# A deep four-layer block on one core: two groups of small matmuls widened from 32 and 56 rows to 128, with the added rows cleared on GpSimd

## Chip, core and metric

One Trainium2 chip, one of its cores. The metric is the device time of one execution of the whole program in microseconds (us); the number compared is the median of several executions.

## What is computed

The input is 16 images of 56 x 56 tokens with 128 channels, in fp32. Four layers follow one another, each as `x = x + layer(group_norm(x))`: a shifted-window attention (7 x 7 windows, 4 heads), a triangle multiplication, a Fourier operator with attention over planes, and a bilinear convolution. The change touches the last two.

In the Fourier layer the 56 image rows are treated as 56 planes. Attention weights between planes are made per head, and one part of the output is a mix of the planes with weights that all pixels share. In the code that is a 56 x 56 matrix `mt`, applied to every column of the image: for each column `j`, `y[:, j] = mt.T @ x[:, j]` for every channel.

In the bilinear layer the reference does this first:

```python
xp = jax.nn.silu(x @ W1) @ W2          # W1: 128 x 160, W2: 160 x 160
q = xp[..., :128]; k = xp[..., 128:144]; v = xp[..., 144:]
q, k, v = l2norm(q per head), l2norm(k), l2norm(v)
```

The 160 hidden channels do not fit 128 partitions, so the kernel holds them as a large part of 128 and a small part of 32. Then `k` and `v` go through grouped 3 x 7 convolutions, and three bilinear products of `q` with their results make the output.

## The kernel before

**Lanes and order.** The 16 images run in two lanes (even and odd images). Each lane has its own arena (128 x 17152 fp32 in SBUF), five `w2` buffers of 128 x 512, eight small ones of 128 x 64 (`sm`), two PSUM banks `psb` and one double bank `psd`. The program is written image by image with plain Python loops; the Tile framework's scheduler then lays the instructions of both lanes out on the engines, by its own timeline of their costs, and sets all waits. Each engine runs its instructions in that order. So a program that differs by a few instructions can be laid out differently throughout.

**The Fourier layer** (`_fourier`, `run` from L1141). After the attention (L1050 to L1133) comes a product with a table of spectral weights: 8 rounds of 8 steps, each step with two table transfers of 56 x 1344 issued by GpSimd (L1200), one product of 112 x 1344 on VectorE (L1202) and a group of matmuls (L368 and L371 are the lines of the helper `together`). Then the planes' product with the common weights: for 14 groups of four columns, four transposes on TensorE (L1235), an evacuation by ScalarE that also subtracts the mean (L1237, into 56 rows of a `w2` buffer), four matmuls with `mt` (L1240, 56 rows) and a copy back (L1241). `mt` is made at L1181. The inverse transforms and two spectral operators end the layer (L945 to L1021, L1245 to L1271).

**The bilinear layer** (`_bilinear`). An image is seven chunks of 448 tokens. `project(q)` (L1317 to L1371) normalizes a chunk on VectorE (L1320), multiplies with `W1` in two parts of 128 and 32 rows of output (L1324), applies Silu on ScalarE (L1325) into `ha` (128 rows) and `hb` (32 rows), and multiplies with `W2`: first for the 128 channels of `q`, over 128 rows (L1327) and over 32 rows (L1328), accumulating in PSUM; then, for four blocks of 112 tokens, for the 32 channels of `k` and `v`, over 128 rows (L1337) and over 32 rows (L1338), with the sums of squares per head next to them (L1339). The `q` part goes to DRAM eightfold (`dy`, L1313), and `k`, `v` after normalization go to a padded image in DRAM; its border comes from a clearing on GpSimd (L1360). `spread` (L1375) loads the padded image back, `conv` (L1389 and `together`) makes the convolutions, and `contract` reads `dy` back in replicated form (L1408), multiplies on VectorE (L1411) and sums on TensorE. Projections run two chunks ahead of their use.

GpSimd's queue holds the table transfers (L1200), clearings (L520, L526, L658, L973, L974, L1061, L1145, L1250, L1258, L1303, L1360), one copy between partitions per image (L1164) and the small pieces of the window attention's input (L536).

Of the kernel before, what the change touches and what calls it, by code (L numbers as in the profile page):

```python
# [42 lines left out]
P = 128  # L43
T = 56
# [3 lines left out]
CH = 448  # L48
# [156 lines left out]
def _weights(i):  # L205

    g = {k: np.asarray(v) for k, v in i.items()}
    w, early = {}, {}
    w["wqkv"] = g["L0_conv_w_qkv"]
    w["wout0"] = g["L0_conv_w_out"]  # L210
    w["bout0"] = g["L0_conv_b_out"][:, None]
    x, y = np.arange(WIN) // WS, np.arange(WIN) % WS
    pb = g["L0_conv_pos_emb"][x[None] - x[:, None] + WS - 1, y[None] - y[:, None] + WS - 1]
    pos = np.zeros((P, WIN), np.float32)
    pos[:WIN] = pb
    pos[64 : 64 + WIN] = pb
    early["pos"] = pos

    pw, gw = g["L1_conv_p_in_w"].T, g["L1_conv_g_in_w"].T
    cut = [slice(0, 64), slice(128, 192)], [slice(64, 128), slice(192, 256)]  # L220
    for n, (a, b) in zip("ab", cut):
        w["w1" + n] = np.concatenate([pw[:, a], pw[:, b], gw[:, a], gw[:, b]], 1)
    w["pout"] = g["L1_conv_p_out_w"].T
    w["gout"] = g["L1_conv_g_out_w"].T
    names = ["ln_in_w", "ln_in_b", "ln_out_w", "ln_out_b"]
    w["ln"] = np.stack([g["L1_conv_" + n] for n in names], 1)

    rows = [e[0] for e in ENT]
    for n, key in (("a", "L2_conv_wQ"), ("b", "L2_conv_wK")):
        k = g[key][:, 0]  # L230
        s = np.concatenate([k[0][:, :12], k[1]], 1)
        for c, part in enumerate("ri"):
            e = s[..., c][:, rows].reshape(32, 32, 2, 8).transpose(2, 1, 0, 3)
            e = np.stack([e, e], 1)
            early[n + part] = e.reshape(P, 256)
            m = s[:, [t[0 if n == "a" else 1] for t in MIR], 0, c].T
            early[n + "m" + part] = np.concatenate([m, m, m, m], 0)
    wq, wk = g["L2_conv_wQs"][:, 0], g["L2_conv_wKs"][:, 0]

    def rep(v, n):  # L240
        return np.broadcast_to(v, (n,) + v.shape)

    early["wq"], early["wk"] = rep(wq, P), rep(wk, P)
    early["wqh"] = np.concatenate([rep(wq[:16], 64), rep(wq[16:], 64)], 0)
    early["wkh"] = np.concatenate([rep(wk[:16], 64), rep(wk[16:], 64)], 0)
    early["bq"] = rep(g["L2_conv_bQs"], P)
    head = np.array([[16 * (s % 2) + 2 * (s // 2) + hh for s in range(16)] for hh in range(2)])
    wv, wp = g["L2_conv_wVs"][:, 0], g["L2_conv_wPs"][0]
    early["wvp"] = np.repeat(wv[head], T, 0)
    early["wpp"] = np.repeat(wp[head], T, 0)  # L250
    early["cols"] = np.stack([wv, wp], 1)
    sc = [g["L2_conv_norm_g"], g["L2_conv_norm_b"]]
    sc += [g["L2_conv_" + n].reshape(-1) for n in ("wM0s", "bM0s", "wM1s", "bM1s", "bPs")]
    w["sc"] = rep(np.concatenate(sc), P)
    for n, key in (("w0", "L2_conv_wM0"), ("w1", "L2_conv_wM1")):
        k = g[key][:, 0, 0]
        s = np.concatenate([k[0][:24], k[1]], 0)
        for c, part in enumerate("ri"):
            w["m" + n + part] = np.concatenate([s[..., c], s[..., c]], 0)
    k = g["L2_conv_wP"][:, :, 0]  # L260
    s = np.concatenate([k[0][:, :24], k[1]], 1)
    v = np.zeros((32, T, 32, 2), np.float32)
    v[:, :16, :16] = g["L2_conv_wV"][0, 0]
    v[:, 40:, :16] = g["L2_conv_wV"][1, 0]
    neg = (-np.arange(T)) % T
    late = {}
    for c, part in enumerate("ri"):
        late["p" + part] = s[..., c].transpose(0, 2, 1).reshape(32, -1)
        late["v" + part] = v[..., c].transpose(0, 2, 1).reshape(32, -1)
        early["vm" + part] = v[:, neg, 0, c]  # L270

    w["l3w1"] = g["L3_conv_W1"]
    w["l3w2a"] = g["L3_conv_W2"][:128]
    w["l3w2b"] = g["L3_conv_W2"][128:]
    h1 = g["L3_conv_H1_w"].reshape(16, 16, 3, 7)
    h2, gg = g["L3_conv_H2_w"][:, 0], g["L3_conv_G_w"][:, 0]

    wk3, wg3 = (np.zeros((P, 4, 2, 4, 8), np.float32) for _ in range(2))  # L280
    wf3 = np.zeros((P, 4, 16, 8), np.float32)
    for u in range(16):
        rows = slice(u % 4 * 21, u % 4 * 21 + 21)
        wk3[rows, u // 4, :, u % 4] = h1[u].reshape(2, 8, 21).transpose(2, 0, 1)
        wg3[rows, u // 4, :, u % 4] = gg.reshape(2, 8, 21).transpose(2, 0, 1)
        wf3[rows, u // 4, :, u % 8] = h2.reshape(16, 21).T
    wk3[84] = g["L3_conv_P1"][0].reshape(4, 4, 2, 8).transpose(0, 2, 1, 3)
    wg3[84] = g["L3_conv_I"][0].reshape(4, 4, 2, 8).transpose(0, 2, 1, 3)
    for n, v in (("l3wk", wk3), ("l3wf", wf3), ("l3wg", wg3)):
        w[n] = v.reshape(P, -1)  # L290
    return w, early, late
# [437 lines left out]
def _fourier(env):  # L729
    e = _Env(env)  # L730
    nc, mm, tt, ts, ptt, act, C, W, bc = e.nc, e.mm, e.tt, e.ts, e.ptt, e.act, e.C, e.W, e.bc
# [409 lines left out]
    def run(b, xt):  # L1141
# [14 lines left out]
        for g in range(8):  # L1156
            p = e.psb()
# [16 lines left out]
        p = e.psb()  # L1174
# [3 lines left out]
        p = e.psb()  # L1178
        mm(p[:T, :T], lhsT=C("fold"), rhs=r[:TT, :T], start=True, stop=True)
        mt = e.sm()  # L1180
        stt(mt[:T, :T], p[:T, :T], scol[:T, 0:1], C("ident")[:T, :T], ALU.mult, ALU.add)  # L1181


# [4 lines left out]
        for q in range(8):  # L1188
            s = slice(q * STEP, (q + 1) * STEP)
# [6 lines left out]
            for two in range(8):  # L1196
# [8 lines left out]
                for p, k, m in ((pa, 0, 2 * STEP), (pb, 2 * STEP, STEP)):  # L1205
                    for half in (1, 0):
# [4 lines left out]
                                lhsT=at[:, pair % 8, pair // 8, :],  # L1211
                                rhs=prods[half][:, k : k + m],
                                start=two == 0,
                                stop=two == 7,
# [3 lines left out]
            c0, o = e.w2(), e.w2()  # L1218
# [4 lines left out]
            p = pb[:TT, 256 : 256 + STEP]  # L1223
# [8 lines left out]
        for g in range(T // 4):  # L1232
            p = e.psb()
            for i in range(4):
                nc.tensor.transpose(p[:T, i * P : (i + 1) * P], y3[:, 4 * g + i, :], C("ident"))  # L1235
            xj = e.w2()
            act(xj[:T, :], p[:T, :], AF.Identity, bias=less[:T])  # L1237
            p = e.psb()
            for i in range(4):
                mm(p[:, i * T : (i + 1) * T], lhsT=xj[:T, i * P : (i + 1) * P], rhs=mt[:T, :T], start=True, stop=True)  # L1240
            nc.scalar.copy(y3[:, 4 * g : 4 * g + 4, :], p[:, : 4 * T].rearrange("p (j t) -> p j t", t=T))  # L1241

        def residual(t0, p):
# [32 lines left out]
def _bilinear(env):  # L1276
    e = _Env(env)
    nc, mm, tt, ts, act, C, W, bc = e.nc, e.mm, e.tt, e.ts, e.act, e.C, e.W, e.bc
# [18 lines left out]
    def run(b, xt):  # L1297
# [12 lines left out]
        def kept(p):  # L1310

            t, d = e.w2(), e.dram()
            nc.scalar.copy(t[:, :CH], p[:, :CH])  # L1313
            nc.scalar.dma_start(out=d.rearrange("p (k t) -> p k t", k=8), in_=bc(t[:, :CH], 1, 8))
            return d

        def project(q):  # L1317

            xg = e.w2()
            ts(xg[:, :CH], xt[:, q * CH : (q + 1) * CH], nm, rs, ALU.add, ALU.mult)  # L1320
            ha, hb = e.w2(), e.w2()
            for t, o, m in ((ha, 0, 128), (hb, 128, 32)):
                p = e.psb()
                mm(p[:m, :CH], lhsT=W("l3w1")[:, o : o + m], rhs=xg[:, :CH], start=True, stop=True)  # L1324
                act(t[:m, :CH], p[:m, :CH], AF.Silu)  # L1325
            p = e.psb()
            mm(p[:, :CH], lhsT=W("l3w2a")[:, :P], rhs=ha[:, :CH], start=True, stop=False)  # L1327
            mm(p[:, :CH], lhsT=W("l3w2b")[:, :P], rhs=hb[:32, :CH], start=False, stop=True)  # L1328
            dq = kept(p)
            sq = e.w2()  # L1330
            act(sq[:, :CH], p[:, :CH], AF.Square)
# [1 line left out]
            p = e.psb()  # L1333
            for a in range(4):
                s = slice(a * TT, (a + 1) * TT)
                o = p[:TT, a * 32 : (a + 1) * 32]
                mm(o, lhsT=ha[:, s], rhs=W("l3w2a")[:, P:], start=True, stop=False)  # L1337
                mm(o, lhsT=hb[:32, s], rhs=W("l3w2b")[:, P:], start=False, stop=True)  # L1338
                mm(p[:TT, P + a * NH : P + (a + 1) * NH], lhsT=sq[:, s], rhs=C("heads"), start=True, stop=True)  # L1339
            sk = e.w2()  # L1340
            act(sk[:TT, :P], p[:TT, :P], AF.Square)
# [13 lines left out]
            p = e.psb()  # L1355
# [93 lines left out]


        queries, kern, feat = {q: project(q) for q in range(2)}, {}, {}
        spread(0, 0)
        for q in range(NCH + 4):
# [42 lines left out]
```

## Time and profile before

| | us |
|---|---|
| median of 3 runs | 13443.8 |
| lowest and highest of them | 13435.75, 13488.92 |
| the profiled execution, its own time | 13405.75 |
| span of the profiled execution, first to last instruction | 13403.8 |
| busy: TensorE, its weight loads, VectorE | 10585.8, 5860.7, 9623.6 |
| busy: ScalarE, GpSimd | 3845.7, 1426.4 |

The mean granted clock of TensorE was 0.847 of full speed. HBM moved 155 GB/s over the span. One pair of images (both lanes) takes about 1650 us, and the span shows that pattern eight times.

How to read it: PE is TensorE's matmuls, PEld its weight loads, which overlap them; DVE is VectorE, ACT ScalarE, POOL GpSimd, SP the queue that issues most transfers. A group's row gives the source line, the engine and operation, the output and inputs by name, for a matmul rows times columns of the stationary operand, the shape of the moving one, and the number of instructions; then the busy time in us, the mean of one in ns, the idle time of the engine just before them, and what ended most of it. An fp32 matmul appears as two instructions (two passes).

### The profile page before, as it was taken

What the parts mean: (1) busy time and instruction counts of PE and PEld (TensorE: products, weight loads), DVE (VectorE), ACT (ScalarE), POOL (GpSimd) and SP (SyncE); (2) the same over time, 40 slices, a digit from 0 to 9 for tenths busy, and PEclk for the clock granted to TensorE, in tenths of its full rate; (3) what the DMA queues carried; (4) which work ended last, traced back from release to release, by engine and by line L of the source; (5) the groups of instructions that cost most, each with busy time, mean ns of one, the idle gap of its engine ahead of it and who ended that gap; (6) DMA issues with size and microseconds to landing.
All of it is one profiled execution on the core that took longest, in us unless ns stands there. A gap on an engine that the chain in (4) does not pass through costs nothing. (4 is left out here: it accounts for less than half of the span.)

```text
span 13403.8 us, 202422 instructions
## 1 busy us (share of the span) xinstructions
PE 10585.8 (79%) x82624; PEld 5860.7 (44%) x82624; DVE 9623.6 (72%) x13985; ACT 3845.7 (29%) x6638; POOL 1426.4 (11%) x2746
## 2 busy tenths in 40 slices
PE   7887687876878778887778877888778887788776
PEld 4454254542544335443355433554335443354432
DVE  7776868667677686676766667767777677866776
ACT  3223141321423224232242222422224232242221
POOL 0120002200022000220002200022000220002200
PEclk9988898878988889888888778888888888888887
DMA  1256904468044680447804468044780447704577
GB/s 35 73 164 230 315 1 118 118 244 300 1 124 124 237 294 9 118 138 240 276 10 118 131 228 291 13 118 130 245 279 10 118 136 252 270 7 118 131 249 267
DMA packets 1091758, 2105.94 MB, mean 157 GB/s; under 512 B 98320, under 2 KB 974096, under 8 KB 1089680
## 3 DMA queue, kind: packets, MB, share of 16 engines
q1 hardware_dynamic: 560000, 823.95, 18.7%
q0 software_dynamic: 165120, 629.61, 17.1%
q10 hardware_dynamic: 365712, 639.44, 13.2%
q8 instruction: 654, 10.72, 0.3%
q14 instruction: 272, 2.23, 0.1%
HBM read 1412.73 MB, written 667.03 MB: 155 GB/s over the span
## 5 line engine op out<-in xcount | busy, mean ns | idle before, releaser
L1411 DVE TENSOR_TENSOR arena<-arena 128x1792 f32<-128x1792 f32 x1344 | 2661.8, 2018 | 724.6 <-DMA arena<-dy 329.5
L1202 DVE TENSOR_TENSOR arena<-arena 112x1344 f32<-112x1344 f32 x1024 | 1569.5, 1552 | 356.8 <-DMA arena<-table 341.1
L371 PE MATMUL psb<-arena,cst 128*32 128x448 f32 x9792 | 1578.0, 672 | 0.0
L368 PE MATMUL psb<-arena,cst 128*32 128x448 f32 x1408 | 818.8, 670 | 799.9 <-DVE arena L1411 750.3
L1200 POOL DMA_DIRECT2D arena<-table x2048 | 1063.7, 521 | 2799.3 <-PE psb L1116 724.8
L371 PE MATMUL psb<-arena 112*64 112x224 f32 (+2 forms) x4864 | 1245.2, 525 | 0.0
L368 PE MATMUL psb<-arena 112*64 112x448 f32 (+1 forms) x1280 | 691.4, 625 | 369.2 <-DVE arena L1093 187.5
L371 PE MATMUL psd<-arena 112*64 112x224 f32 (+1 forms) x3072 | 749.4, 465 | 0.0
L368 PE MATMUL psd<-arena 112*64 112x448 f32 x1024 | 554.5, 627 | 211.4 <-DVE arena L1202 190.9
L1093 DVE TENSOR_TENSOR arena<-w,coef 128x1792 f32<-128x1792 f32 x256 | 507.6, 2020 | 210.7 <-PE psb L371 187.4
L371 PEld LDWEIGHTS psb<-arena 112*64 112x64 f32 (+1 forms) x4864 | 435.6, 153 | 509.7 <-issue 507.3
L368 PEld LDWEIGHTS psb<-arena,cst 128*32 128x32 f32 x1408 | 118.4, 119 | 1154.3 <-DVE arena L1411 869.2
L678 PE MATMUL psd<-wgt,arena 128*64 128x128 f32 x7168 | 514.4, 293 | 112.4 <-DVE arena L690 96.5
L371 PEld LDWEIGHTS psb<-arena,cst 128*32 128x32 f32 x9792 | 367.6, 125 | 471.4 <-issue 451.0
L1396 ACT COPY arena<-psd 128x896 f32<-128x896 f32 x336 | 303.4, 905 | 930.8 <-DVE arena L1411 549.4
L678 PEld LDWEIGHTS psd<-wgt,arena 128*64 128x64 f32 x7168 | 450.0, 145 | 217.1 <-issue 129.2
L907 PE MATMUL psb<-cst,arena 128*128 128x64 f32 (+1 forms) x2688 | 454.9, 341 | 92.4 <-ACT arena L917 63.2
L371 PE MATMUL psd<-arena,wgt 128*32 128x448 f32 x2688 | 500.6, 604 | 34.4 <-DMA arena<-padded 34.0
L907 PEld LDWEIGHTS psb<-cst,arena 128*128 128x128 f32 x2688 | 437.2, 254 | 148.8 <-ACT arena L917 74.0
L1313 ACT COPY w<-psb 128x448 f32<-128x448 f32 x336 | 178.6, 532 | 1089.1 <-PE psb L371 761.8
L368 PE MATMUL psd<-arena,wgt 128*32 128x448 f32 x896 | 438.6, 607 | 42.4 <-DMA arena<-padded 37.4
L371 PEld LDWEIGHTS psd<-arena 112*64 112x64 f32 x3072 | 287.0, 151 | 284.4 <-issue 283.0
(299 smaller groups left out, 19594.2 us busy)
## 6 DMA issues: line engine op xcount, KB each, us to landing
arena<-table POOLq DMA_DIRECT2D x2048, 294.0 KB, 8.7
dy<-w ACTq DMA_DIRECT2D x336, 1792.0 KB
arena<-dy SPq DMA_DIRECT2D x1344, 448.0 KB
arena<-padded SPq DMA_DIRECT2D x896, 162.8 KB
w<-x SPq DMA_DIRECT2D x112, 224.0 KB
out<-w SPq DMA_DIRECT2D x112, 224.0 KB
padded<-w ACTq DMA_DIRECT2D x336, 62.0 KB
arena<-arena POOLq DMA_DIRECT2D x16, 784.0 KB, 9.8
```

What stands on the lines that cost most here:

```text
L368: done = mm(**first)
L371: mm(**kw)
L678: mm(p[half : half + 64, i // 4, i % 4 * P : (i % 4 + 1) * P], lhsT=xh[:, c0 : c0 + 64], rhs=W(w).rearrange("p (k c) -> p k c", c=64)[:, : ...
L907: mm(p[:, 2 * i * nl : 2 * (i + 1) * nl], lhsT=src[:, t * P : (t + 1) * P], rhs=fc, start=True, stop=True)
L1093: tt(t4, bc(ys[c][:, l0 : l0 + 4, :], 1, 8), bc(coef[:, c, h0 : h0 + 8, l0 : l0 + 4], 3, T), ALU.mult,)
L1200: nc.gpsimd.dma_start(out=t[hh * T : (hh + 1) * T, :], in_=bc(tflat[q, two, hh], 0, T))
L1202: tt(t4, bc(x3[:, :, s], 1, 2), t4, ALU.mult)
L1313: nc.scalar.copy(t[:, :CH], p[:, :CH])
L1396: nc.scalar.copy(z, p[:, :, :CH])
L1411: tt(t4, bc(rep, 2, 2), bc(z, 1, 2), ALU.mult)
```

## The change

Three places get all 128 rows. The small part of `W2` is padded on the host with 96 rows of zeros, which changes the contents of the weight array and not its size. The buffers that carry the other operand, or both, are cleared by GpSimd before ScalarE or VectorE writes their 32 or 56 rows: `hb` (448 columns, 112 times), `xj` (512 columns, 224 times) and `mt` (64 columns, 16 times). The matmuls L1240, L1328 and L1338 then run over 128 rows. What is added to their sums is zero times zero.

```diff
-    w["l3w2b"] = g["L3_conv_W2"][128:]
+    w["l3w2b"] = np.pad(g["L3_conv_W2"][128:], ((0, 96), (0, 0)))
...
         mt = e.sm()
+        nc.gpsimd.memset(mt, 0.0)
         stt(mt[:T, :T], p[:T, :T], scol[:T, 0:1], C("ident")[:T, :T], ALU.mult, ALU.add)
...
             xj = e.w2()
+            nc.gpsimd.memset(xj, 0.0)
             act(xj[:T, :], p[:T, :], AF.Identity, bias=less[:T])
             p = e.psb()
             for i in range(4):
-                mm(p[:, i * T : (i + 1) * T], lhsT=xj[:T, i * P : (i + 1) * P], rhs=mt[:T, :T], start=True, stop=True)
+                mm(p[:, i * T : (i + 1) * T], lhsT=xj[:, i * P : (i + 1) * P], rhs=mt[:, :T], start=True, stop=True)
...
             ha, hb = e.w2(), e.w2()
+            nc.gpsimd.memset(hb[:, :CH], 0.0)
...
-            mm(p[:, :CH], lhsT=W("l3w2b")[:, :P], rhs=hb[:32, :CH], start=False, stop=True)
+            mm(p[:, :CH], lhsT=W("l3w2b")[:, :P], rhs=hb[:, :CH], start=False, stop=True)
...
-                mm(o, lhsT=hb[:32, s], rhs=W("l3w2b")[:, P:], start=False, stop=True)
+                mm(o, lhsT=hb[:, s], rhs=W("l3w2b")[:, P:], start=False, stop=True)
```

Line numbers below are those of the kernel before unless said otherwise; those of the changed kernel are one to three higher from `mt` on.

## The prediction

> **What bounds the kernel now.** I read the page first, then the groups by shape, the instructions in order of time inside one projection, the windows of one pair of images, and the waits. The page first (busy time by engine, tenths in 40 slices, two groups):
>
> ```profile
> PE 10585.8 (79%) x82624; PEld 5860.7 (44%) x82624; DVE 9623.6 (72%) x13985; ACT 3845.7 (29%) x6638; POOL 1426.4 (11%) x2746
> PE   7887687876878778887778877888778887788776
> DVE  7776868667677686676766667767777677866776
> L1411 DVE TENSOR_TENSOR arena<-arena 128x1792 f32<-128x1792 f32 x1344 | 2661.8, 2018 | 724.6 <-DMA arena<-dy 329.5
> L368 PE MATMUL psb<-arena,cst 128*32 128x448 f32 x1408 | 818.8, 670 | 799.9 <-DVE arena L1411 750.3
> ```
>
> No engine is full: TensorE is busy 79% of the span and VectorE 72%, in every slice alike, and the longest waits point at each other. TensorE's matmuls wait 750 us for the products of L1411; L1411 waits 330 us for the transfers that feed it. So two lanes, two engines and the DMA queues hand the end to one another, and a saving on one engine comes through only in part. The small matmuls that the change touches:
>
> ```profile
> L1338 PE MATMUL psb<-wgt,w 32*112 32x32 f32 x896 | 190.9, 295 | 0.0
> L1337 PE MATMUL psb<-wgt,w 128*112 128x32 f32 x896 | 183.3, 289 | 0.0
> L1240 PE MATMUL psb<-sm,w 56*128 56x56 f32 x1792 | 328.9, 340 | 65.9 <-ACT w L1237 65.4
> L1360 POOL MEMSET w<- 32x496 f32 x112 | 56.7, 506 | 3224.3 <-PE psb L1337 1740.5 <-PE psb L1338 1116.4 <-issue 148.3
> ```
>
> An fp32 matmul stands as two passes, so x896 is 448 matmuls. Durations overlap here; what a pass takes of the engine is the distance between starts. Inside one projection, in order of time (start, us, line, two passes a row):
>
> ```profile
> 1068.30 0.36 PE L1337 MATMUL psb<-wgt,w 128*112 128x32 f32 x2
> 1068.59 0.38 PE L1338 MATMUL psb<-wgt,w 32*112 32x32 f32 x2
> 1068.90 0.36 PE L1339 MATMUL psb<-cst,w 128*112 128x8 f32 x2
> 1069.12 0.36 PE L1337 MATMUL psb<-wgt,w 128*112 128x32 f32 x2
> ```
>
> From L1337 over L1338 and L1339 to the next L1337 it is 0.29 + 0.31 + 0.22 = 0.82 us. The step without a change of rows (L1339 to L1337) is the short one, though L1339 itself came after a change. Pass by pass over the whole trace (medians of start to start): L1339 to L1337 98 ns; L1337 to L1338 193; between L1338's two passes 119; L1338 to L1339 188; L1339's two passes 119. Thus a change of rows costs about 94 ns at the border and 21 ns in the pass behind it.
>
> **What the Trainium skill says.** "TensorEngine Tiling (Array Packing)", Key Properties: changing the tiling mode, not just the tile, drains TensorE. The trace agrees: 188 to 193 ns at a border against 98. "TensorE: Matmul & The Clock Gate", LDWEIGHTS (loading the stationary operand): loading goes by columns, and a 32-row load takes as long as a 128-row one. The trace agrees: L1338's load of 32 rows has a median of 171 ns, L1337's of 128 rows 178. So the added rows cost TensorE nothing. "GPSIMD Engine Reference", Specifications: GpSimd shares its SBUF interfaces with VectorE and contends with instructions of two SBUF inputs. The trace shows no price for that here: 35 of the L1411 products lay beside a clearing and took 2017 ns at the median, the other 1309 took 2018.
>
> **The change part by part.** *Projection, removed.* Per chunk there are four rounds of L1337, L1338, L1339. Each loses (193-98) + (119-98) + (188-98) + (119-98) = 227 ns, in all 0.91 us. L1328's second pass starts 480 ns after the first, where same-mode passes of 448 columns (L989, L1389) stand at 375 or 376: 0.105 us. From L1328 to L1337 it is 464 ns against the same 375: 0.09 us, and 0.02 us in the pass behind. Sum 1.12 us a chunk, and 112 chunks (16 images of 7) make 125 us of TensorE. The built programs give a second count: neighbouring matmuls of different tile shape fall from 5092 to 4027; 1065 times 0.115 us is 122 us. I take 125. At the lower clock it is more, so I let it reach 140.
>
> *Planes' product, removed.* L1240 goes from 64 rows to 128, but its neighbour L1235 loads 56 columns and stays in a mode of 64 columns, so most borders stay borders. Of the 1065 only some 75 are left for it: 9 us at most, I take 0.
>
> *Added on GpSimd.* Clearings of 448 columns at 0.462 us (L973) times 112, of 512 at about 0.52 (L1360, 496 columns, 0.506) times 224, of 64 at about 0.15 (L1061) times 16: 52 + 117 + 2 = 171 us on an engine that is 11% busy. Beside other work that is nothing; the waits count.
>
> *Wait of the planes' evacuation (L1237) for its clearing.* The five w2 buffers of a lane let a clearing run four groups ahead; the fourteen evacuations of an image lie over 50 to 86 us after the first pair, so about 4 us a group and some 16 us ahead. Behind L1237 on ScalarE stand the other lane's copies, and L1240 waits for it. Taken at 0; if that cover is gone it is the slower rival below. In the built order the clearings are mostly one run per image; 21 stand directly behind a table transfer of the other lane, and 22 such transfers directly behind a clearing. Where table transfers wait longer, L1202, which waits 341 us for them now, waits more.
>
> *Wait of the small Silu (L1325) for its clearing.* Behind it on ScalarE is the whole projection's chain and the other lane's evacuations; L1328 waits for it. Today L1325 waits for a buffer freed by a transfer (dy, padded) for 44.5 + 43.7 + 35.6 = 124 us in 23 stretches. Where that buffer is hb, the clearing (0.46 us and a hand-over of about 0.1) comes in between: 23 times 0.56 is 13 us. Bounds: 0 (all were ha's) and 112 times 0.56 = 63 us (every time). I take 10. Twelve of these clearings stand near L520, which clears the next image's arena and must wait for the last product of the lane before. From the third pair on, L520 ran 14, 24, 31, 34 and 38 us before the Silu in question, so that queue is clear in time.
>
> *Added on ScalarE.* The built order has 163 loads of function tables against 158; 5 times 1.283 us is 6 us on an engine 29% busy: 2 us. The mt clearing comes long before its use: 0.
>
> *Reordering.* The scheduler lays the program out anew: 22% of TensorE's instructions change their relative place, by 8 places at the median. But the lanes stand to each other as before: when lane 0 enters the projection, lane 1 has issued 0.66, 0.64, 0.56 and then five times 0.54 of its VectorE work, in both programs. Between starts of L1303 the pairs take 1620 to 1704 us, a scatter of 28 us; eight independent draws would be 80 us, and with the lanes unmoved I allow half, plus or minus 40.
>
> *How much of 125 us comes through.* The windows of 2700 to 3300 us, where the second pair projects:
>
> ```profile
> 2700.00:2800.00 100.00, 83.93 (x561) 51.63 (x560) 50.43 (x114) 40.42 (x75) 2.50 (x6) 0.81 0.47 161
> 2900.00:3000.00 100.00, 80.36 (x472) 34.49 (x468) 69.81 (x90) 19.52 (x34) 1.52 (x3) 0.80 0.99 352
> 3100.00:3200.00 100.00, 71.56 (x456) 26.45 (x448) 78.25 (x59) 14.37 (x22) 0.51 (x1) 0.81 0.89 313
> ```
>
> (columns: length, busy us of PE, PEld, DVE, ACT, POOL, granted clock, DMA share, GB/s.) Where the projections begin, TensorE is 84% busy and DMA half idle; later DMA stands at 0.89 to 0.99 and a faster TensorE only waits sooner for dy. Behind a projection's block TensorE is idle 2.1 us at the median within the next 10 us, more than the 1.1 us saved; only 11% of the blocks are followed by 10 us without idle time. About half the chunks lie in the early part, with most of a saving felt there and little later: I take 40%, 50 us, with 20% and 100% as ends. What is late next is the L1411 product and its dy transfer.
>
> Sum: -50 + 10 + 2 = -38 us on the profiled execution, whose span is 13403.8 and whose time 13405.75: 13,368. The median of the runs shown is 13443.8, 1.0028 of that; so I forecast 13,405, or -0.3%.
>
> **The rivals.** *TensorE bounds the projections.* For: 80 to 84% busy, and blocks of the projection hold up the other lane's matmuls on the same in-order engine. Against: the idle time behind the blocks. Then all of 125 comes through and the rest costs 10: 13,290 profiled, 13,328 median.
>
> *GpSimd's queue couples the lanes (slower).* Where clearings and table transfers alternate, mainly in the first two pairs, a clearing waits for a buffer of one lane with the other's transfers behind it, and the reverse. A table transfer that waits for psd waits 314.7 us in 110 stretches, 2.9 us each; 43 such places make 125 us. It decides once a clearing is held longer than the 16 us it runs ahead. Against: L1200 waits are short of that but for a few (longest 21.9 us), and most clearings stand in unbroken runs. Then -50 + 12 + 125 = +87: 13,493 profiled, 13,530 median.
>
> *The change doesn't do what it says.* The pauses would belong to something else than the rows (a fresh set of weights, the short moving operand), and stay with 128 rows. Against: L1339 to L1337 changes weights too and has no pause. Then only the 12 us of costs: 13,456.
>
> **How the numbers follow.** Part of the gain (13,405): 0.45. All of it (13,328): 0.27. Coupling (13,530): 0.18. No effect (13,456): 0.10. About 0.5%, 67 us, is what a measurement of this kernel can tell from no change, so the borders are 13,377 and 13,511. Faster: 0.27 and 0.05 of the first case's spread, 0.32. Slower: most of the coupling, 0.16, and 0.05 of the spread of the others, 0.21. Same: 0.47. The range runs from 13,305, most of the full gain, to 13,530, the middle of the coupling.
>
> **What would show it.** L1337, L1338 and L1339 should start every 0.20 us, L1328's passes 375 ns apart, and TensorE's busy time should fall while its idle time before L368 grows by more than half of that. L1237 and L1325 should show no long wait for POOL. Wrong I am if ScalarE waits for POOL by tens of us, if L1202's wait for the table grows well over 341 us, or if L1411 waits less for TensorE by a hundred.

## The result, and the profile after

The changed kernel took 13243.7 us (median of 4 runs, 13231.6 to 13296.5) beside 13466.1 us for the kernel before in the same runs: a ratio of 0.985, 95% interval 0.982 to 0.988, so 1.5% faster. Run again later, it gave 0.989 (0.985 to 0.993). The forecast was -0.3%, with 13,305 as the lower end of the range: the time lies below it.

The page of the changed kernel, whose profiled execution was the slowest of its four (13296.46 us, span 13294.5, granted clock 0.856 against 0.847); first the busy time of each engine, then the two groups that stood for the coupling of TensorE and VectorE:

```profile
PE 10334.9 (78%) x82624; PEld 5712.3 (43%) x82624; DVE 9627.8 (72%) x13985; ACT 3845.1 (29%) x6643; POOL 1624.1 (12%) x3098
...
L1414 DVE TENSOR_TENSOR arena<-arena 128x1792 f32<-128x1792 f32 x1344 | 2659.5, 2019 | 693.9 <-DMA arena<-dy 314.5
...
L368 PE MATMUL psb<-arena,cst 128*32 128x448 f32 x1408 | 807.3, 661 | 812.8 <-DVE arena L1414 729.8
```

TensorE is busy 251 us less, GpSimd 198 us more, VectorE and ScalarE as before. TensorE's idle time ahead of L368 has grown by 13 us only: the saving did not turn into waiting there. Elsewhere a part of it did. Between the two profiled executions the span fell by 109 us, so TensorE's idle time as a whole (span less busy time) rose by 142 us, from 2818 to 2960. Half of that rise stands ahead of L589, in the window attention, far from the change; first before, then after:

```profile
L589 PE MATMUL psb<-cst,arena 128*49 128x128 f32 x2048 | 329.0, 310 | 77.4 <-DVE arena L584 47.1 <-ACT arena L581 9.7 <-ACT arena L591 7.8
```

```profile
L589 PE MATMUL psb<-cst,arena 128*49 128x128 f32 x2048 | 348.7, 328 | 152.8 <-DVE arena L584 93.7 <-ACT arena L581 36.8 <-DVE sm L405 7.7
```

The two executions make the gain look small: the profiled one of the kernel before (13405.75 us) was faster than each of the four that it is measured by above.

The touched matmuls by shape (lines are now 2 to 3 higher: L1337, L1338, L1339 are L1340, L1341, L1342, and L1240 is L1242; L1239 evacuates the planes):

```profile
L1341 PE MATMUL psb<-wgt,w 128*112 128x32 f32 x896 | 166.6, 269 | 0.0
L1340 PE MATMUL psb<-wgt,w 128*112 128x32 f32 x896 | 158.6, 260 | 0.0
L1242 PE MATMUL psb<-sm,w 128*128 128x56 f32 x1792 | 301.8, 323 | 75.9 <-ACT w L1239 75.5
L1239 ACT ACTIVATE w<-psb,lessmean 56x512 f32<-56x512 f32 x224 | 152.6, 681 | 36.6 <-PE psb L1236 32.7 <-POOL w L1238 1.6 <-POOL arena L1260 0.7
```

L1239 waits 1.6 us in all for its clearing (L1238). One projection in order of time (start, us, line, two passes a row):

```profile
1123.06 0.36 PE L1340 MATMUL psb<-wgt,w 128*112 128x32 f32 x2
1123.26 0.36 PE L1341 MATMUL psb<-wgt,w 128*112 128x32 f32 x2
1123.46 0.34 PE L1342 MATMUL psb<-cst,w 128*112 128x8 f32 x2
1123.65 0.36 PE L1340 MATMUL psb<-wgt,w 128*112 128x32 f32 x2
```

From L1340 to the next L1340 it is 0.59 us where it was 0.82. The next two views show the planes, which the forecast had put at nothing: eight passes of the planes' product and behind them the next group's transposes, first before, then after.

```profile
2395.53 1.10 PE L1240 MATMUL psb<-sm,w 56*128 56x56 f32 x8
2396.55 0.64 PE L1235 MATMUL psb<-cst,arena 128*56 128x128 f32 x4
```

```profile
2440.78 1.10 PE L1242 MATMUL psb<-sm,w 128*128 128x56 f32 x8
2441.72 0.60 PE L1236 MATMUL psb<-cst,arena 128*56 128x128 f32 x4
```

The transposes start 1.02 us after the product before the change and 0.94 us after it: there was a pause at that border, and it is gone. From the last pass to the first transpose it is 202 ns before and 112 after (at full clock).

The waits of GpSimd's clearings and of L1203 (was L1202) for the table; columns are total us, times, longest:

```profile
POOL w L1324 <- DMA dy<-w: 380.4, 30, 34.3
...
DVE arena L1203 <- DMA arena<-table: 380.0, 415, 4.5
...
POOL w L1238 <- PE psb L1242: 367.5, 122, 7.9
```

The clearings wait for buffers, up to 34 us, but hand little on: L1203's wait has grown by 39 us, from 341.

Two sums over whole traces are used below. The *touched time* is the sum of the distances between starts of neighbouring matmuls that both belong to the planes (L1235, L1240) or to the second product of the projection (L1327 to L1339). Waits are left out: distances over 420 ns, or 1,200 ns for the 448-column products, are not counted. It was 1029 us before and 791 after, 238 less. In the traces the granted clock of TensorE stands either at full speed or at half. The *half-clock share* is the share of the passes L1337, L1338 and L1339 that started while it stood at half: 24% before, 5% after. A pass that starts 98 ns behind its like at full clock takes 187 ns there. Both sums look at the touched matmuls alone. The clock can change for the others too, so TensorE's busy time and the half-clock time of a whole trace (4092 us before, 3839 after) are given where they tell something else.

### The profile page after: what moved, and what is told of

Its sections match the earlier page's. It is cut to its first block, busy times and chain, and to the rows that moved or that the text cites. A ratio compares the mean times of both kernels' runs of the same rounds, so it can differ in the third digit from the quotient of the medians.

```text
span 13294.5 us, 203312 instructions
## 1 busy us (share of the span) xinstructions
PE 10334.9 (78%) x82624; PEld 5712.3 (43%) x82624; DVE 9627.8 (72%) x13985; ACT 3845.1 (29%) x6643; POOL 1624.1 (12%) x3098
## 5 line engine op out<-in xcount | busy, mean ns | idle before, releaser
L1414 DVE TENSOR_TENSOR arena<-arena 128x1792 f32<-128x1792 f32 x1344 | 2659.5, 2019 | 693.9 <-DMA arena<-dy 314.5
L1203 DVE TENSOR_TENSOR arena<-arena 112x1344 f32<-112x1344 f32 x1024 | 1569.9, 1552 | 394.8 <-DMA arena<-table 380.0
L371 PE MATMUL psb<-arena,cst 128*32 128x448 f32 x9792 | 1556.4, 662 | 0.9 <-ACT arena L629 0.9
L368 PE MATMUL psb<-arena,cst 128*32 128x448 f32 x1408 | 807.3, 661 | 812.8 <-DVE arena L1414 729.8
L371 PE MATMUL psb<-arena 112*64 112x224 f32 (+2 forms) x4864 | 1278.8, 535 | 0.0
L368 PE MATMUL psb<-arena 112*64 112x448 f32 (+1 forms) x1280 | 716.0, 646 | 377.6 <-DVE arena L1093 191.6
L371 PE MATMUL psd<-arena 112*64 112x224 f32 (+1 forms) x3072 | 776.8, 480 | 0.0
L368 PE MATMUL psd<-arena 112*64 112x448 f32 x1024 | 573.1, 646 | 186.4 <-DVE arena L1203 171.9
L368 PEld LDWEIGHTS psb<-arena,cst 128*32 128x32 f32 x1408 | 119.7, 120 | 1179.6 <-DVE arena L1414 864.3
L907 PE MATMUL psb<-cst,arena 128*128 128x64 f32 (+1 forms) x2688 | 430.2, 330 | 93.0 <-ACT arena L917 71.4
L368 PE MATMUL psd<-arena,wgt 128*32 128x448 f32 x896 | 440.7, 610 | 67.3 <-DMA arena<-padded 42.6
L907 PEld LDWEIGHTS psb<-cst,arena 128*128 128x128 f32 x2688 | 415.6, 244 | 136.1 <-ACT arena L917 80.6
L589 PE MATMUL psb<-cst,arena 128*49 128x128 f32 x2048 | 348.7, 328 | 152.8 <-DVE arena L584 93.7
```

What stands on the lines that cost most here:

```text
L368: done = mm(**first)
L371: mm(**kw)
L589: nc.tensor.transpose(p[:WIN, i * P : (i + 1) * P], s3[:, 4 * g + i, :], C("ident"))
L907: mm(p[:, 2 * i * nl : 2 * (i + 1) * nl], lhsT=src[:, t * P : (t + 1) * P], rhs=fc, start=True, stop=True)
L1203: tt(t4, bc(x3[:, :, s], 1, 2), t4, ALU.mult)
L1414: tt(t4, bc(rep, 2, 2), bc(z, 1, 2), ALU.mult)
```

## The experiments

No kernel leaves work out; e5 and e8 repeat some. Ratios are to the kernel before, run beside them on the same chip. Touched time is in us.

| run | median us | ratio (95%) | touched time | half-clock share |
|---|---|---|---|---|
| e1 clearings alone | 13549.6 | 1.009 (1.006 to 1.013) | 1078 | 32% |
| e2 projection alone | 13261.5 | 0.989 (0.985 to 0.992) | 855 | 3% |
| e3 planes alone | 13353.0 | 0.994 (0.992 to 0.996) | 968 | 22% |
| e4 `mt` clearing alone | 13509.0 | 1.006 (1.002 to 1.009) | 1036 | 28% |
| e5 sums three times | 13458.4 | 1.001 (0.999 to 1.003) | 993 | 18% |
| e6 small part of 112 rows | 13276.7 | 0.989 (0.984 to 0.993) | 805 | 7% |
| e7 72 rows | 13328.3 | 0.992 (0.989 to 0.996) | 842 | 14% |
| e8 clearings twice | 13294.6 | 0.990 (0.984 to 0.996) | 817 | 11% |
| e9 narrow rows, grouped | 13518.7 | 1.007 (1.005 to 1.009) | 898 | 20% |
| e10 the same and wide planes | 13463.6 | 1.002 (1.000 to 1.004) | 876 | 24% |
| e11 order control | 13425.9 | 1.000 (0.998 to 1.002) | 1064 | 30% |
| e12 changed kernel again | 13284.5 | 0.989 (0.985 to 0.993) | 794 | 6% |
| e13 pieces alone | 13312.1 | 0.991 (0.987 to 0.994) | 932 | 23% |
| e14 query alone | 13347.6 | 0.995 (0.993 to 0.997) | 962 | 12% |

**The parts apart.** e1: all three clearings, rows as before.

```diff
-    mm(..., lhsT=hb[:, s], rhs=W("l3w2b")[:, P:], ...)
+    mm(..., lhsT=hb[:32, s], rhs=W("l3w2b")[:32, P:], ...)
     (L1331 and L1242 back to 32 and 56 rows in the same way)
```

> The three clearings stay, but L1242, L1331 and L1341 run over 56 and 32 rows as in the kernel before. Theory A (the pauses of TensorE at a change of rows are what was saved): no gain is left, ratio to the kernel before 0.998 to 1.006, about 13,440 to 13,540 us, L1340 to L1341 again 193 ns. Theory B (the scheduler's new order makes most of the gain): the program is laid out anew here as well, so about half of the gain or more stays, ratio 0.993 or below.

e2 widens the projection alone, with the clearing of `hb`.

> Only the projection is widened and only hb is cleared. Theory A: 125 us of TensorE at full clock are saved here and nearly all of it comes through, ratio 0.988 to 0.992. Theory of the prediction (40% comes through): 0.996. Theory B (order): anything, not tied to this part.

e3 widens the planes' product alone, with the clearings of `xj` and `mt`.

> Only the planes' product is widened, with mt and xj cleared. Theory A with the border of 203 ns gone as in the trace of the changed kernel, 135 ns in each of 224 groups, 30 us at full clock and up to 45 with the lower one: ratio 0.996 to 0.998. The prediction took 0 for this part: ratio 1.000 to 1.002. Theory B: anything.

e4 is the kernel before with 16 clearings of `mt` and nothing else, which makes the scheduler lay the program out anew.

> The kernel before with nothing but the 16 clearings of mt, 2 us of GpSimd; the scheduler moves about as many instructions of TensorE against each other as in the changed kernel (9,800 of 43,522). Theory A: ratio 0.997 to 1.003. Theory B (order): 0.5% or more off 1 in either direction.

Measured: -1.1% and -0.6% for the two widenings, which add up to the whole within the intervals; so neither part is nothing, the planes included. The touched time falls by 174 us in e2 and by 61 in e3, together 235 of the 238. e1 and e4 are 0.9 and 0.6% slower, though e4 adds 16 short clearings only: a new order alone can cost that. The granted clock goes with it. Over all executions its mean was 0.838 in e1 and 0.842 in e4, beside 0.846 for the kernel before in the same runs, and 0.856 and 0.853 in e2 and e3. By and large, over all the runs here, a lower mean clock goes with a longer time. Whether a worse order lowers the clock by idle time, or the lower clock makes the time, is not shown.

**Does TensorE time in the projection come through?** e5: the sums per head three times in place of once.

```diff
+                for _ in range(3):
                     mm(p[:TT, P + a * NH : ...], lhsT=sq[:, s], rhs=C("heads"), start=True, stop=True)
```

> The changed kernel, with the sums per head (L1342, 128x8) written three times in place of once: 1792 more passes in the projections, each 98 ns start to start in a row of equal tiles at full clock, so 1792 x 98 ns = 176 us more TensorE time, no mode change, no new wait. Theory A (TensorE time in the projections goes into the end one to one): about 176 us more than the changed kernel, 1.3%, less or more by 60 us for the new order. Theory B (as predicted: 40% comes through, the rest meets idle time): about 70 us more, 0.5%, same scatter. The page will show how much of it stands as more busy time and how much as less idle time of PE.

Measured: 1.001 against the changed kernel's 0.985 and 0.989, so 1.3 to 1.6% or 168 to 218 us more (each plus or minus some 60), for 202 us more touched time (993 - 791). In the profiled executions TensorE's busy time rose by 280 us (10334.9 to 10614.5) and the span by 218. So the larger part of added TensorE time comes through: 40% would be 81 us of the touched time, or 112 of the busy time. Whether all of it does is not shown, for the order is a new one here too.

**The clearings and the rows.** e6 does without `hb`'s clearings: `W1` gets 80 columns of zeros and the small part is made 112 rows high.

```diff
-            nc.gpsimd.memset(hb[:, :CH], 0.0)
-            for t, o, m in ((ha, 0, 128), (hb, 128, 32)):
+            for t, o, m in ((ha, 0, 128), (hb, 128, 112)):
     (the padding of the weights and hb[:112] in L1331 and L1341 left out here)
```

> The changed kernel without the 112 clearings of hb: the first weight is padded with 80 columns of zero, so that the small part of the hidden layer is made 112 rows high, and its pieces in the second product are 112 rows high as well. The 32-column tile of L1327 goes too: 148 fewer neighbouring matmuls of different tile shape, by 0.117 us = 17 us of TensorE; 52 us of GpSimd and 112 places where the small Silu waits for GpSimd go. The Silu has more rows, the same columns: nothing. Theory A (all TensorE time counts): 15 to 30 us less than the changed kernel, 0.1 to 0.2%. Theory C (the clearings are what cost the 0.6 to 0.9% of the runs without wider rows): as hb's clearings are a third of them and sit in ScalarE's chain, 40 us or more less.

e7 has 72 rows in place of 128 in the three places (`hb[:72]`, `xj[:72]`, `mt[:72]`).

> The changed kernel with 72 rows in place of 128 in the three places (small part, its key and value pieces, planes' product): same clearings, same tiles as the tile shape goes by the program (128x128), no mode change. Theory D (the higher granted clock comes from the pauses being gone): as the changed kernel within 0.5%, and the share of these passes at half clock stays at some 6% in the projection and 30% in the planes. Theory E (it comes from the number of rows that are fed): the share goes up towards the 23% and 43% of before, the granted clock falls to about 0.85, and the time is 50 us or more above the changed kernel.

e8 writes each clearing of `xj` and `hb` twice.

> The changed kernel with each clearing of xj and hb written twice: 336 more clearings, 170 us more on GpSimd (11 to 12% busy). Theory A (clearings lie beside other work): within 0.5% of the changed kernel, order scatter alone. Theory C (the clearings cost the 0.9% that the kernel with clearings and narrow rows lost): about 120 us more, and longer waits of ScalarE for POOL, or of VectorE L1203 for the table.

Measured: e6 and e8 cannot be told from the changed kernel (0.989 and 0.990 beside 0.985 and 0.989). The clearings cost nothing that shows within the intervals (some 0.6%), neither when taken away nor when doubled, and e6 gained nothing to be seen. e7 is between: its tiles are those of the changed kernel and nothing pauses, yet the half-clock share is 14% where the four kernels with 112 or 128 rows (after, e12, e6, e8) have 5 to 11%, and its ratio is 0.3 to 0.7% higher. That leans to the rows, but not by much more than the scatter.

**Pauses without wide rows.** e9 keeps 32 rows and clears nothing; it groups the pieces by their rows, behind a product with zeros that opens the PSUM bank.

```diff
+            mm(p[:TT, :160], lhsT=C("ident")[:16, 16:128], rhs=W("l3w2a")[:16, :160], start=True, stop=False)
+            for h, w2, k in ((hb, "l3w2b", 32), (ha, "l3w2a", 128)):
+                for a in range(4):
+                    s = slice(a * TT, (a + 1) * TT)
+                    mm(p[:TT, a * 32 : (a + 1) * 32], lhsT=h[:k, s], rhs=W(w2)[:, P:], start=False, stop=False)
     (the four sums follow in a loop of their own; the old loop is gone)
```

> The kernel before, rows left narrow and nothing cleared, but the projection's key and value pieces grouped by their rows: a product with zeros (16 rows, 160 columns) opens the bank, then the four 32-row pieces, then the four 128-row pieces, then the four sums. Counted in the built program with transposes as full tiles, neighbouring matmuls of different tile shape fall from 5241 to 4432: 809 x 0.115 us = 93 us of TensorE less, 112 zero products of about 0.28 us = 31 us more, net 62 us less at full clock. Both theories: some 60 us less, 0.4%, with 60 us either way for the new order. Theory D (the pauses are what lowers the granted clock): the 32-row passes stand at half clock in 10% or less, and 30 to 60 us come on top. Theory E (it is the number of rows fed): they stay at 20% or more, and nothing comes on top.

e10 adds the wide planes and their clearings to it.

> The grouped projection of the run before and the planes' product over 128 rows with its clearings (xj, mt), hb not cleared. Tile changes counted the same way 5241 to 4087: 1154 x 0.115 us = 133 us less, zero products 31 us more, net 102 us less, 0.8%, with 60 us either way for the order. If the clearings of hb and the wait of the small Silu were dear, this would be as fast as the changed kernel, 1.5% below the kernel before, or faster; if wide rows bring something beyond the absent pauses, it stays 0.5% or more behind the changed kernel.

e11 is a second control of the order: one column of `xj` cleared, rows as before.

> The kernel before with one column of xj cleared by GpSimd ahead of each planes' evacuation, rows left narrow: almost no work (224 short clearings), but the scheduler lays the program out anew. Tile changes 5241 to 5363: 122 x 0.115 us = 14 us more. Theory F (a new order alone is a scatter about nothing of 0.5%): between 50 us less and 80 us more. Theory G (every new order of this tuned program costs 0.5 to 0.9%, as in the two runs with narrow rows so far): 70 to 120 us more.

e12 is the changed kernel itself.

> The changed kernel itself once more, beside the others on the same chip: 1.5% below the kernel before, within 0.4%. It gives the footing for the comparisons of these runs.

Measured: e9 missed. Its touched time is 131 us less, and it is 0.7% slower. Its page:

```profile
PE 10564.8 (78%) x82848; PEld 5870.6 (44%) x82848; DVE 9618.8 (71%) x13985; ACT 3894.4 (29%) x6670; POOL 1441.8 (11%) x2746
```

TensorE's busy time fell by 21 us only, so that some 110 us came back in other matmuls, and the clock stood at half for 4195 us of the trace against 4092. The program is in a quite different order (by the traces, half of VectorE's instructions stand 21 places or more from where they were; 2 in the changed kernel), so e9 does not say whether the order or the narrow rows took the gain back. e10 is 0.4% faster than e9, which fits the planes' part, and stays 1.4 to 1.7% behind the changed kernel, which e12 puts at 0.989; its order is a new one again, and it tells no more. e11 is as fast as the kernel before: with narrow rows a new order cost between nothing and 0.9%.

**The split, with the order held.** e13 widens the pieces alone; the built program has TensorE's, VectorE's and ScalarE's instructions in the order of the kernel before, but for a few (nine in ten are in their very place or one from it). e14 widens the query's product alone; its order is that of e2 in the same sense. The cuts are against the changed kernel; in both the planes are as in the kernel before.

```diff
 e13:
-            mm(p[:, :CH], lhsT=W("l3w2b")[:, :P], rhs=hb[:, :CH], start=False, stop=True)
+            mm(p[:, :CH], lhsT=W("l3w2b")[:32, :P], rhs=hb[:32, :CH], start=False, stop=True)
 e14:
-                mm(o, lhsT=hb[:, s], rhs=W("l3w2b")[:, P:], start=False, stop=True)
+                mm(o, lhsT=hb[:32, s], rhs=W("l3w2b")[:32, P:], start=False, stop=True)
```

> The kernel before with 128 rows only in the key and value pieces (L1338 there), L1328 left at 32 rows, hb cleared. The built program keeps the order of the kernel before almost instruction for instruction, so no order scatter enters. Tile changes, transposes counted as full tiles, 5241 to 4396: 845 x 0.115 us = 97 us of TensorE at full clock. One to one: about 95 us less, 0.7%. As predicted (40%): about 40 us less, 0.3%. Clock: these pieces stream only 32 columns each, so a rule by rows times columns streamed predicts that the share of half clock in the projection falls little below its 23%; a rule by pauses predicts some 6%.

> The kernel before with 128 rows only in the query's small part (L1328 there, 448 columns), the key and value pieces left at 32 rows, hb cleared. The built program has the order of the run with the whole projection widened (e2), so the two differ by 827 tile changes, 95 us at full clock, and the rows of the 32-column pieces. One to one: e2's 1.1% gain shrinks to 0.4%. As predicted (40%): to 0.8%. Clock: by rows times columns streamed, the query's 2 x 448 columns are most of what the change added, so the share of half clock in the projection stays below 12%; by pauses it goes back towards 23%.

Measured: e13 is 0.9% faster (0.6 to 1.3), 126 us (79 to 173) for 97 us less touched time. This is the cleanest run of the study: the same order, the clearing of `hb` included, the pauses of the pieces gone. 40% of the touched time would have been 39 us. But the touched time is not all that TensorE saved. The page of e13:

```profile
PE 10413.4 (78%) x82624; PEld 5743.4 (43%) x82624; DVE 9615.6 (72%) x13985; ACT 3845.0 (29%) x6639; POOL 1483.0 (11%) x2858
```

TensorE's busy time fell by 172 us (from 10585.8), 75 more than the touched time. The half-clock share of the touched passes stays at 23%, yet the half-clock time of the whole trace fell from 4092 to 3898 us, among others in matmuls of the Fourier layer: the share of L945's passes (L945 here too) fell from 23 to 14%, that of L907's from 44 to 38. The mean clock of all seven executions, 0.852 beside 0.847, says the same. So 126 us is more than the touched saving and 0.73 of the busy saving; 40% of either (39 or 69 us) lies below the interval. In the trace of e13 the pieces follow each other as in the changed kernel (lines one higher than in the kernel before):

```profile
2903.66 0.36 PE L1338 MATMUL psb<-wgt,w 128*112 128x32 f32 x2
2903.86 0.36 PE L1339 MATMUL psb<-wgt,w 128*112 128x32 f32 x2
2904.05 0.34 PE L1340 MATMUL psb<-cst,w 128*112 128x8 f32 x2
2904.25 0.36 PE L1338 MATMUL psb<-wgt,w 128*112 128x32 f32 x2
```

In e14 they still pause:

```profile
1043.84 0.36 PE L1338 MATMUL psb<-wgt,w 128*112 128x32 f32 x2
1044.13 0.38 PE L1339 MATMUL psb<-wgt,w 32*112 32x32 f32 x2
1044.44 0.36 PE L1340 MATMUL psb<-cst,w 128*112 128x8 f32 x2
1044.66 0.36 PE L1338 MATMUL psb<-wgt,w 128*112 128x32 f32 x2
```

Yet it is 0.5% faster (0.3 to 0.7), 73 us, though its absent pauses are worth 22 us at full clock (0.195 us a chunk). Its touched time fell by 68 us: the other 46 are mostly passes that now run at full clock, since the half-clock share went from 24 to 12%. Beside the kernel before, its order is another one. Against e2, in the same order, it is 0.6% slower (plus or minus 0.4), for 107 us more touched time.

## Why the prediction was wrong

The direction of the mechanism was right: narrow rows between wide ones pause TensorE, and wide rows take the pauses away. Three steps of the sum failed. Two made TensorE's saving too small: the prediction put it at 125 us, and TensorE's busy time fell by 251. The third, the share of it that reaches the end, was too low as well. Together they hid three quarters or more of the gain.

**"The planes' product: I take 0".** Wrong. The reason given, that L1235 "loads 56 columns and stays in a mode of 64 columns", does not hold for transposes: from L1242's last pass to the first transpose (128 x 56) it is 112 ns, as between passes of one kind, while from a product of 56 rows it is 202. So a transpose of 56 columns is no change of mode behind a 128 x 128 product. The Trainium skill, "TensorEngine Tiling (Array Packing)", Gotcha 2: Feature Incompatibilities, lists the fp32 transpose among what column tiling excludes, which fits. The prediction's second count had the same fault. Its 5092 and 4027 changes of tile shape take these transposes for narrow tiles; with fp32 transposes as full tiles the orders in the traces have 5241 and 3851, which is 1390 fewer, not 1065, and 160 us at 0.115 us each, not 122. Group by group the planes' eight passes and transposes lose 135 ns at full clock, 30 us over 224 groups; with the clock the touched time of e3 falls by 61 us, and the time by 0.6% (86 us).

**"125 us of TensorE", "at the lower clock it is more, so I let it reach 140".** For the projection the count of pauses was right, but for one border left out, L1327 to L1328 (469 ns before, 376 after, 10 us at most). e13's 97 us is what 845 borders at 0.115 us give, and L1328's passes went from 464 and 480 to 376 ns as said. What was missed is that the clock itself would change. The pauses of the whole change are worth 160 us at full clock; by subtraction, the other 90 or so of the 251 are matmuls that moved to full clock, and pauses that had stood at half clock, where they lasted longer. Of e2's 174 us of touched time, 125 are the pauses and 49 are of this kind; the same reckoning leaves 31 of e3's 61. In e13 75 us lie outside the touched matmuls altogether.

What moves the clock, the runs show in part. The Trainium skill, "TensorE: Matmul & The Clock Gate", What's actually happening: the default is throttled, and activity in windows of some 3.4 us releases it. The trace agrees: the clock changes only at multiples of 3.41 us. The question is what counts as activity. Weigh every streamed column of the kernel before by the part of the 128 x 128 array that its tile covers, rows and columns in steps of 32, and sum it up in each window. After a full-clock window with less than 1,100, the next is at full clock in 9% of 353 cases, with over 2,000 in nearly all of 1677; after a half-clock window with less than 1,100 in 7% of 546, with over 1,600 in 85% of 411. One threshold tells what comes after a half-clock window in 84% of the cases, and in 77% if the columns are not weighed. But this gain comes from the columns of the tile: weighed by them alone it is 84% too, and by the rows alone 77%. So the count does not show that rows matter.

Something else speaks for the rows. All eight kernels with 32 rows in the query's product (448 columns) have a half-clock share of 20% or more, e13 among them; the seven with more rows there have 3 to 18%. The expectations of e13 and e14 said so beforehand, 23% and 12% beside 24%. Yet no two runs in the same order differ in the query's rows alone. And from e14 to e2, which do share their order, the share falls from 12 to 3% when the pieces are widened, so pauses or the pieces' rows have a part too. That rows of zeros count as activity is therefore likely and not shown.

**"I take 40%, 50 us".** Too low, and its sign did not come. The prediction read idle time behind the projections' blocks as time that a faster TensorE would only lengthen, and named idle time before L368 growing by more than half of the saving: it grew by 13 us. L1414's wait for TensorE hardly moved (279.5 before, 290.7 after). In e13, in the same order, 126 us came of 97 (touched) or 172 (busy); in e5 168 to 218 of 202 or 280. For the whole change it is 150 to 222 us (by the two measurements) of 238 or 251, so 0.6 to 0.93. The two profiled executions alone give 109 of 251, 0.43, with the 142 us of new idle time shown above. So a part of the saving did turn into waiting, as the prediction said, though elsewhere and less of it; how large that part is stays open between these figures, since orders differ and that alone is worth up to 0.9%. With 40% of 251 us the saving would have come to 100 us, short of both medians. The rival that took TensorE to bound the projections was nearer on the share, with the same 125 us.

**The rest of the sum.** GpSimd's 171 us beside other work at nothing: right as far as can be seen (198 measured busy; ScalarE waited 14 us in all for the clearings, 6.6 at the longest; doubled in e8, still nothing that shows). Wait of the small Silu, 10 us: none for GpSimd stands in the trace of the changed kernel. L1237's wait, 0: 1.6 us. Table loads 158 to 163: so it is. L1202's wait, 341: 380, which is 39 us more. Reordering, plus or minus 40 us: too small. The controls with narrow rows gave 0, +0.6 and +0.9%, up to 120 us, so a range for this program laid out anew has to carry about that much.

**The rivals.** The coupling by GpSimd's queue did not come: L1324's clearings are held up to 34 us, longer than the 16 us that the text named as its point, but the product behind the table transfers waited only 39 us more. "The change doesn't do what it says" is out by the starts every 0.20 us.

## What to carry to other kernels

Count the changes of tile shape in the built order, with fp32 transposes as full tiles, and price each from the distance between starts in the trace (here 0.115 us); and do not write a saving down for idle time that only follows it: here six tenths or more of TensorE's saving came through by the medians, though no engine was busy for more than 79% of the span. Ask of any matmul whose shape or pauses change what that does to the granted clock of the whole program, not only to itself: a ledger of the touched matmuls alone missed 75 us of 172 in e13. To tell a small effect from a new order, look for an edit that leaves the built order as it was; if there is none, run a control that changes the order alone.

## What the runs showed of the hardware

- A change between tiles of 128 and 32 rows cost 94 ns at full clock and 117 at half (304 against 187 from L1337 to L1338), and 21 ns more in the pass behind it at both.
- 128 x 56 fp32 transposes behave as a full tile: no pause behind a 128 x 128 product (112 ns), a pause behind one of 56 rows (202 ns).
- The projection's passes stood at half clock in 22 to 32% with 32 rows in the query's product (kernel before, e1, e3, e4, e11, e13; 20 and 24% with the pieces grouped, e9 and e10), 14% with 72, 3 to 11% with 112 or 128 (with the pieces widened too and the sums written once), and 12 and 18% in e14 and e5.
- Time and mean granted clock moved together over the runs: 0.838 in e1 (+0.9%), 0.842 in e4 (+0.6%), 0.846 to 0.847 in the kernel before, 0.852 in e13 (-0.9%), 0.858 in the changed kernel (-1.5%). Which of the two leads is not shown.
- Clearings of 448 and 512 columns on GpSimd, even twice over, showed no cost within some 0.6% beside a VectorE that is 72% busy: 1764.5 us of GpSimd's time in e8 against 1624.1 in the changed kernel, ratios 0.990 and 0.985 to 0.989.
